# Four layer-1 weights and the centering matrix kept in SBUF for all images, in the room of one of two silu(z) buffers

## The chip, the core and the metric

The kernel runs on one core of a Trainium2 chip, as one program that handles all four images. The metric is the device time of that program in microseconds, the median of repeated runs. One execution was profiled; its trace gives every instruction of the five engines (TensorE = PE, VectorE = DVE, ScalarE = ACT, GpSimd = POOL, SyncE = SP) and the DMA packets.

## The reference

Four layers, applied one after the other to `x` of shape (4 images, 64, 64, 128), all in float32:

```python
# layer 0: four-direction selective scan (DI=256 channels, N=16 states, K=4 directions, L=4096 tokens)
xz = ln(x) @ in_proj;  x_, z = split(xz);  xc = silu(depthwise_conv3x3(x_) + conv_b)
# per direction k: delta, Bs, Cs are projections of xc
h = exp(delta*A) * h + (delta*xc) * B          # along 4096 tokens, per channel and state
y_k = sum_n(h * C) + D*xc                      # the four directions are summed
x = x + (ln(y) * silu(z)) @ out_proj;  x = x + fc2(gelu(fc1(ln(x))))
# layer 1: attention over all 4096 positions, softmax over the query axis
f, g, hv = x@Wq, x@Wk, x@Wv;  x = gamma * (hv^T @ softmax(f g^T, axis=1)) + x
# layer 2: 1x1 and 3x3 convolutions, batch norm, hard-swish, two residual blocks
# layer 3: 7x7 neighborhood attention, 4 heads, then an MLP
```

## The kernel before, in words

**Stages.** `scan_inputs` (lines 307 to 417) makes an image's inputs for the scan, in eight chunks of 512 tokens: layer norm, projection, convolution, `silu(z)` into the tile `sz` (line 389), `silu` of the convolution into `xc`, then `delta`, `B`, `C` and the product `du` (line 358, GpSimd). Each is stored to DRAM. `sz` is stored from ScalarE's DMA queue at line 412 and read back much later by `scan_output`.

`selective_scan` (487 to 611) runs the recurrence of an image, direction by direction. Its smallest step is a tile of 128 rows by 512 tokens: ScalarE makes `exp(delta*A)` (line 540, in PSUM), GpSimd makes `dB` (534, two tiles in one instruction), VectorE runs the recurrence with one scan instruction (542); the product with `C` is made by VectorE (547) or, for a fixed share of the units, by GpSimd (555); TensorE sums over states into `py` (588). An image has 1024 such VectorE scan instructions, the program 4096. This text counts progress in them: "scan 950" is the place before which 950 of them stand in VectorE's list.

`rest` (1721 to 1730) is everything else of an image: `scan_output` (gate, output projection and MLP of layer 0, together with the layer-3 MLP of the image before), `layer1`, `layer2`, `layer3_attention`. `rest` of image 0 runs during the scan of image 1, and so on. `rest` of image 3 has no scan beside it, and is built in a wider form that uses the scan's memory (`wide`): it is the last part of the program.

**What sets the order.** The kernel is written with the tile framework. The framework orders the instructions of each engine when the program is built, by priorities (`rest` goes ahead of the scan, which fills in) and by an estimate of when operands are ready (`TileContext(nc, schedule_with_timeline_sim=True)`). On the chip each engine then takes its list strictly in that order, and waits at an instruction whose operands are not there. DMA issues on SP stand in such a list too. So an edit in one place can shift how two stages interleave elsewhere.

**Memory.** Tiles come from pools. A pool opened later may lie where a closed pool lay, and a tile's first write then waits for the last use of what was there. `sz` in `scan_inputs` comes from a pool of two buffers.

**What the change touches.** In `scan_output`, each call makes the matrix `center` (identity minus 1/256, two 128x128 blocks, line 632) with a VectorE memset (633) and a VectorE add (634), and loads its weights; `out_proj_b` (631) is two VectorE products of the loaded weights; the first matmuls (651) use `center`, and the first VectorE work on their result is line 656. In `layer1`, each call loads `Wq`, `Wk`, `Wv` and `gamma` with the helper `load` (line 196, four DMA issues on SP) into the pool `l1_big`. The last VectorE instruction of a layer-3 attention tile is line 1443 (`x <- x, pj`), after line 1437 and ScalarE's lines 1414 (softmax exponentials), 1434 and 1435; line 1447 stores the result.

Of the kernel before, what the change touches and what calls it, by code (L numbers as in the profile page):

```python
# [28 lines left out]
F32 = mybir.dt.float32  # L29
# [7 lines left out]
B, H, W, C = 4, 64, 64, 128  # L37
NT = H * W
NJ = NT // 128
DI, NS, R, KD = 256, 16, 8, 4  # L40
ND = DI // 128
FF = 4 * C
NF = FF // 128
LC = 512
# [145 lines left out]
    return out  # L190


def loader(tc, pool, A, layer):
    def load(name, shape, src=None):
        t = pool.tile(shape, F32, name=f"w{layer}_{name}")
        tc.nc.sync.dma_start(t, A[f"L{layer}_conv_{name}"] if src is None else src)
        return t

    return load
# [107 lines left out]
def scan_inputs(tc, K, A, D, img):  # L307
# [4 lines left out]
    nc = tc.nc  # L312
    with ExitStack() as ctx:
        pool = ctx.enter_context(tc.tile_pool(name="si_a", bufs=2))
        wpool = ctx.enter_context(tc.tile_pool(name="si_aw", bufs=1))
        psum = ctx.enter_context(tc.tile_pool(name="si_ap", bufs=4, space=PSUM))
        load = loader(tc, wpool, A, 0)
# [46 lines left out]
        for c in range(NCH + 1):  # L364
            acts = []
            if c < NCH:
                xt = pool.tile([128, 4, 128], F32, name="x")
                nc.sync.dma_start(xt, token_tiles(A["x"][img], c))
                xnT = pool.tile([128, LC], F32, name="xnT")
                layernorm_T(tc, K, pool, psum, xt, ln_w, ln_b, xnT)  # L370
                band = pool.tile([128, ND, RC + 2, W], F32, name="band", bufs=3)
                bands[c] = band
                for d in range(ND):
                    ps = psum.tile([128, LC], F32, name="ps")
                    nc.tensor.matmul(ps, in_proj[:, d * 128 : (d + 1) * 128], xnT, start=True, stop=True)
                    rows = ps.rearrange("p (h w) -> p h w", w=W)
                    nc.scalar.copy(band[:, d, 1 : RC + 1, :], rows)
                    if c > 0:
                        nc.scalar.copy(bands[c - 1][:, d, RC + 1, :], rows[:, 0, :])
                        nc.scalar.copy(band[:, d, 0, :], bands[c - 1][:, d, RC, :])  # L380
                sz = pool.tile([128, ND, LC], F32, name="sz")
                for d in range(ND):
                    ps = psum.tile([128, LC], F32, name="ps")
                    mm = nc.tensor.matmul(
                        ps, in_proj[:, DI + d * 128 : DI + (d + 1) * 128], xnT, start=True, stop=True
                    )
                    if d == 0:
                        together.open(mm)
                    acts.append(lambda d=d, ps=ps, sz=sz: nc.scalar.activation(sz[:, d, :], ps, AF.Silu))
            if c > 0:  # L390

                b, src = c - 1, bands.pop(c - 1)
                top, bottom = (1 if b == 0 else 0), (RC + 1 if b == NCH - 1 else RC + 2)
                for d in range(ND):
                    ps = psum.tile([128, LC], F32, name="ps")
                    mm = conv3x3(
                        nc,
                        ps.rearrange("p (h w) -> p h w", w=W),
                        lambda t, d=d: diag[:, d, t, :],
                        src[:, d, top:bottom, :],  # L400
                        1 - top,
                        RC,
                        bottom - top,
                    )
                    acts.append(
                        lambda d=d, ps=ps, b=b: nc.scalar.activation(
                            xc[:, d, span(b)], ps, AF.Silu, bias=conv_b[:, d : d + 1]
                        )
                    )
            together.run(mm, acts)  # L410
            if c < NCH:
                nc.scalar.dma_start(D.sz[img][c], sz)
            if c > 0:
                nc.scalar.dma_start(D.xc[img][c - 1], xc[:, :, span(c - 1)])
                steps(0, c - 1)
# [198 lines left out]
def scan_output(tc, K, A, D, img, xT, last, scan_over=None):  # L614
# [5 lines left out]
    nc = tc.nc  # L620
    with ExitStack() as ctx:
        side = "left" if scan_over is None else "right"
        pool = ctx.enter_context(tc.tile_pool(name="so", bufs=2, side=side))
        wpool = ctx.enter_context(tc.tile_pool(name="so_w", bufs=1, side=side))
# [4 lines left out]
        out_proj_b = wpool.tile([128, ND, C], F32, name="out_proj_b")  # L629
        for d in range(ND):  # L630
            nc.vector.tensor_scalar_mul(out_proj_b[:, d, :], out_proj[:, d, :], onorm_b[:, d : d + 1])
        center = wpool.tile([128, ND, 128], F32, name="center")
        nc.vector.memset(center, -1.0 / DI)
        nc.vector.tensor_add(center[:, 0, :], center[:, 0, :], K.ident)
        ln_w, ln_b = load("ln2_w", [128, 1]), load("ln2_b", [128, 1])
        P = load_mlp(load)
        together = Together(tc, K)
# [126 lines left out]
def layer1(tc, K, A, D, img, xT, wide):  # L764
# [6 lines left out]
    with ExitStack() as ctx:  # L771
        big = ctx.enter_context(tc.tile_pool(name="l1_big", bufs=1))
        pool = ctx.enter_context(tc.tile_pool(name="l1", bufs=1))
        psum = ctx.enter_context(tc.tile_pool(name="l1_p", bufs=1, space=PSUM))
        load = loader(tc, big, A, 1)
        Wq, Wk, Wv = load("Wq", [128, 32]), load("Wk", [128, 128]), load("Wv", [128, C])
        gamma = load("gamma", [128, 1])
        L1 = SimpleNamespace()
        L1.f = f = big.tile([128, 2, LC], F32, name="l1_f")
        L1.g = g = big.tile([128, NCH, LC], F32, name="l1_g")  # L780
# [970 lines left out]
def network(tc, A, out):  # L1751
    nc = tc.nc
    with ExitStack() as ctx:
        nc.scalar.preload_act_table_set("natural_log_exp_and_others")
        K = make_consts(ctx, tc)
        dram = ctx.enter_context(tc.tile_pool(name="scratch", bufs=1, space=DRAM))

        def scratch(name, shape, kind=F32):
            return dram.tile(shape, kind, name=f"{name}_dram")

        D = SimpleNamespace()
        D.bias = scratch("bias", [len(BIAS_KINDS), 128, HEADS * 512])
        D.biasT = [[scratch(f"biasT{k}_{i}", [128, HEADS, LC]) for i in range(4)] for k in range(3)]
        D.T = scratch("T", [128, HEADS * (2 * KW - 1) + 1, W])
        D.conv_diag = scratch("conv_diag", [128, ND, 9, 128])
        D.w2_norms = scratch("w2_norms", [128, len(NORMS2), 4])
        D.w2_cv4, D.w2_bias = scratch("w2_cv4", [128, 128]), scratch("w2_bias", [3, 128], BF16)
        for name, shape in (("sz", [128, ND, LC]), ("xc", [128, ND, LC]), ("y", [128, ND, LC])):
            setattr(D, name, [[scratch(f"{name}{b}_{c}", shape) for c in range(NCH)] for b in range(B)])
        for name, shape in (("delta", [128, ND, LC]), ("du", [128, ND, LC]), ("bc", [NS, 2, LC])):  # L1770
            made = [
                [[scratch(f"{name}{b}_{k}_{c}", shape) for c in range(NCH)] for k in range(KD)] for b in range(B)
            ]
            setattr(D, name, made)
        D.y_first = [[[scratch(f"y_first{b}_{k}_{c}", [128, ND, LC]) for c in range(NCH)] for k in range(2)] for b in range(B)]
        D.y_cols = [scratch(f"y_cols{b}", [NCH, 128, NCH, ND, RC * RC]) for b in range(B)]
        for name in ("x4", "x5"):
            setattr(D, name, [scratch(f"{name}_{b}", [NT, C]) for b in range(B)])
        D.shift = [scratch(f"shift{b}", [NJ, 128]) for b in range(B)]

        with ExitStack() as scan_ctx:
            S = make_scan(scan_ctx, tc, K, A)
            make_conv_diagonals(tc, K, A, D.conv_diag)
            with priority(tc, K, SCAN_FIRST // 2):
                with tc.tile_pool(name="mk_w2", bufs=1, side="right") as pool:
                    make_layer2(tc, K, A, D, pool)
            scan_inputs(tc, K, A, D, 0)
            before = None
            for img in range(B):
                with priority(tc, K, SCAN_FIRST):  # L1790
                    selective_scan(tc, K, S, D, img)
                if img == 0:
                    make_bias(tc, K, A, D)
                    for later in range(1, B):
                        scan_inputs(tc, K, A, D, later)
                    more = scan_ctx.enter_context(tc.tile_pool(name="ss_more", bufs=1))
                    S.products.widen(more, 4)
                    S.inputs.widen(more, 1)
                else:
                    rest(tc, K, A, D, img - 1, before)  # L1800
                    before = img - 1, out[img - 1]
            rest(tc, K, A, D, B - 1, before, scan_ctx.close, out[B - 1])
        needed = ctx.enter_context(tc.tile_pool(name="needed", bufs=1)).tile([1, 1], mybir.dt.int32, name="needed")
        bound_exceeded(tc, K, needed)
        with tc.If(nc.values_load(needed) > 0):
            everything_again(tc, K, A, D, out)
# [80 lines left out]
```

## Time and profile before

| | us |
|---|---|
| median of 3 runs (8716.36 to 8720.45) | 8719.03 |
| the profiled execution's own time | 8713.75 |
| its span, first to last instruction | 8712.4 |
| PE busy (share of the span) | 6971.9 (80%) |
| DVE busy | 7095.9 (81%) |
| ACT busy | 5688.0 (65%) |
| POOL busy | 7119.3 (82%) |

The mean granted TensorE clock was 0.865. A page of the profile gives busy times by engine, the span in 40 equal slices, the chain of work that ended last, and the costliest groups of instructions; the trace answers questions on windows, waits and single instructions. In a row of the timeline the first number is the start in us from the span's start, the second the duration, and what stands in brackets is how long the engine had been idle and what released it. In a row of windows, each engine's busy time within the window is followed by its number of instructions; the last three numbers are the granted TensorE clock, the busy share of the DMA engines and their GB/s. A short name such as `w_fc_w` stands for several tiles, because numbers in names are left out.

### The profile page before, as it was taken

What the parts mean: (1) busy time and instruction counts of PE and PEld (TensorE: products, weight loads), DVE (VectorE), ACT (ScalarE), POOL (GpSimd) and SP (SyncE); (2) the same over time, 40 slices, a digit from 0 to 9 for tenths busy, and PEclk for the clock granted to TensorE, in tenths of its full rate; (3) what the DMA queues carried; (4) which work ended last, traced back from release to release, by engine and by line L of the source; (5) the groups of instructions that cost most, each with busy time, mean ns of one, the idle gap of its engine ahead of it and who ended that gap; (6) DMA issues with size and microseconds to landing.
All of it is one profiled execution on the core that took longest, in us unless ns stands there. A gap on an engine that the chain in (4) does not pass through costs nothing. (4 is left out here: it accounts for less than half of the span.)

```text
span 8712.4 us, 101929 instructions
## 1 busy us (share of the span) xinstructions
PE 6971.9 (80%) x30468; PEld 2615.3 (30%) x30468; DVE 7095.9 (81%) x8477; ACT 5688.0 (65%) x11652; POOL 7119.3 (82%) x3112
## 2 busy tenths in 40 slices
PE   6758587786788878777798877777899877888978
PEld 2223132222422222233322222234322223344333
DVE  4788787788899999998899999998899999913433
ACT  5657676675666676667766676667766766654366
POOL 6989999898899989998899989998899989900000
PEclk8868687787899988888899988888999988899989
DMA  5776667676555556565455566565455565520020
GB/s 181 254 261 236 244 235 257 227 261 220 172 176 167 170 190 206 190 223 186 162 180 169 171 197 201 192 225 176 164 172 168 180 204 196 191 73 5 0 84 11
DMA packets 859647, 1562.73 MB, mean 179 GB/s; under 512 B 224446, under 2 KB 342348, under 8 KB 856781
## 3 DMA queue, kind: packets, MB, share of 16 engines
q1 hardware_dynamic: 728781, 1379.94, 47.8%
q10 hardware_dynamic: 130304, 176.19, 5.7%
q8 instruction: 244, 4.00, 0.2%
q14 instruction: 318, 2.61, 0.1%
HBM read 1286.51 MB, written 281.92 MB: 180 GB/s over the span
## 5 line engine op out<-in xcount | busy, mean ns | idle before, releaser
L534 POOL TENSOR_TENSOR dB<-du,b_rows 128x1024 f32<-128x1024 f32 x2048 | 4797.9, 2367 | 374.9 <-DVE hc L542 95.0
L540 ACT ACTIVATE dA<-dt,w_A_log 128x512 f32<-128x512 f32 x4096 | 2778.3, 690 | 509.9 <-DVE hc L542 256.7
L542 DVE TENSOR_TENSOR_SCAN dA<-dA,state,dB 128x512 f32<-128x512 f32 x2072 | 2559.9, 1272 | 295.9 <-POOL dB L534 140.4
L555 POOL TENSOR_TENSOR hc<-hc,c_rows 128x1024 f32<-128x1024 f32 x864 | 2045.3, 2367 | 73.4 <-issue 22.2
L542 DVE TENSOR_TENSOR_SCAN hc<-dA,state,dB 128x512 f32<-128x512 f32 x1512 | 1871.9, 1267 | 281.8 <-ACT dA L540 123.5
L547 DVE TENSOR_TENSOR hc<-dA,c_rows 128x512 f32<-128x512 f32 x2368 | 1522.6, 675 | 31.8 <-PE py L588 13.9
L588 PE MATMUL py<-hc,pick 128*32 128x512 f32 x8192 | 1231.0, 675 | 261.5 <-POOL hc L555 235.4
L549 ACT COPY state<-dA 128x1 f32<-128x1 f32 x2072 | 318.6, 158 | 1170.8 <-DVE hc L547 1158.9
L878 PE MATMUL pa<-e,l_v 128*128 128x512 f32 x2048 | 1069.5, 654 | 16.6 <-ACT e L834 16.1
L830 PE MATMUL pair<-l_g,l_f 32*128 32x512 f32 x2048 | 533.3, 670 | 172.6 <-ACT e L834 130.6
L834 ACT ACTIVATE e<-pair 128x1024 f32<-128x1024 f32 (+1 forms) x448 | 508.5, 1135 | 234.4 <-PE pair L830 228.0
L1019 POOL MEMSET l_h<- 64x128 f32 x8 | 1.6, 196 | 707.9 <-DVE l_h L993 707.9
L878 PEld LDWEIGHTS pa<-e,l_v 128*128 128x128 f32 x2048 | 376.3, 200 | 673.9 <-issue 624.4
L588 PEld LDWEIGHTS py<-hc,pick 128*32 128x32 f32 x8192 | 212.1, 115 | 996.5 <-issue 467.5
L277 PE MATMUL ps<-band,w_conv_diag 128*128 128x504 f32 (+3 forms) x1152 | 501.9, 595 | 6.4 <-ACT delta L427 5.7
L1404 PE MATMUL pair<-table,ident 128*128 128x512 f32 x768 | 397.3, 641 | 91.7 <-ACT e L1414 63.3
L231 PE MATMUL ps<-ident,ln_xn 128*128 128x128 f32 x512 | 144.4, 375 | 327.6 <-ACT ln_xn L228 243.9
L542 DVE TENSOR_TENSOR_SCAN dA<-dA,dB 128x512 f32<-128x512 f32 x296 | 348.2, 1211 | 45.8 <-ACT dA L540 22.0
L358 POOL TENSOR_TENSOR du<-delta,xc 128x1024 f32<-128x1024 f32 x128 | 333.4, 2614 | 47.7 <-ACT delta L427 46.7
L1414 ACT ACTIVATE e<-pair 128x1024 f32<-128x1024 f32 (+1 forms) x224 | 254.3, 1135 | 95.8 <-PE pair L1408 95.5
L277 PEld LDWEIGHTS ps<-band,w_conv_diag 128*128 128x128 f32 x1152 | 221.1, 193 | 288.0 <-issue 261.1
L830 PEld LDWEIGHTS pair<-l_g,l_f 32*128 32x128 f32 x2048 | 140.0, 189 | 530.2 <-ACT e L834 258.9
(297 smaller groups left out, 8674.4 us busy)
## 6 DMA issues: line engine op xcount, KB each, us to landing
b_rows<-bc_dram SPq DMA_DIRECT2D x1024, 256.0 KB
c_rows<-bc_dram SPq DMA_DIRECT2D x1024, 256.0 KB
dt<-delta_dram SPq DMA_DIRECT2D x512, 512.0 KB
du<-du_dram SPq DMA_DIRECT2D x512, 512.0 KB
delta_dram<-delta ACTq DMA_DIRECT2D x128, 512.0 KB
du_dram<-du SPq DMA_DIRECT2D x128, 512.0 KB
table<-biasT_dram SPq DMA_DIRECT2D x72, 512.0 KB
y_first_dram<-y_sum ACTq DMA_DIRECT2D x128, 256.0 KB
```

The costliest lines, as they stand in the source:

```text
L277: mm = nc.tensor.matmul(out[:, r0 - row0 : r1 - row0, c0:c1], lhsT((dy + 1) * 3 + dx + 1), src[:, r0 + dy : r1 + dy, c0 + dx : c1 + dx], s ...
L358: nc.gpsimd.tensor_mul(du.rearrange("p d (a b) -> p d a b", b=H), deltas[b].rearrange("p d (a b) -> p d a b", b=H), tk,)
L534: nc.gpsimd.tensor_mul(dB, dus[pp], mid(bt, 2))
L540: nc.scalar.activation(dA, dts[pp][:, g, :], AF.Exp, scale=S.A[:, k, j, pr, g : g + 1])
L542: nc.vector.tensor_tensor_scan(hg[:, order], dA[:, order], dB[:, g, order], 0.0 if i == 0 else state[:, j, pr, g : g + 1], ALU.mult, ALU.add,)
L547: mm = nc.vector.tensor_mul(hc[:, g, :], dA, ct)
L555: made.append(nc.gpsimd.tensor_mul(hc, hc, mid(ct, 2)))
L588: mm = nc.tensor.matmul(py[0][32 * q : 32 * q + 32, :], S.pick, hcs[q // 2][:, q % 2, :], start=(k == 1 and j == 0), stop=(j == NJS - 1),)
L830: nc.tensor.matmul(ps[:, u, :], f[quad, t // 4, span(t % 4, 128)], g[quad, c, :], start=True, stop=True)
L834: made = nc.scalar.activation(e, ps, AF.Exp)
L878: nc.tensor.matmul(pa, v[:, 8 * q + t, :], es[q], start=(t == 0 and q == 0), stop=(t == 7 and q == 3),)
L1404: nc.tensor.matmul(ps[:, u, :], K.ident, t[:, u, :], start=True, stop=False)
```

## The change

`center`, `Wq`, `Wk`, `Wv` and `gamma` are made or loaded once, right after the constants, into a pool that stays open for the whole program. `layer1` and `scan_output` use these tiles. In `scan_inputs`, `sz` has one buffer where it had two: 4096 bytes a partition are given back there, and the new pool takes 2180 (1024 for `center`, 1156 for the four weights).

```diff
+def make_resident(ctx, tc, K, A):
+    pool = ctx.enter_context(tc.tile_pool(name="resident", bufs=1))
+    K.center = pool.tile([128, ND, 128], F32, name="center")
+    tc.nc.vector.memset(K.center, -1.0 / DI)
+    tc.nc.vector.tensor_add(K.center[:, 0, :], K.center[:, 0, :], K.ident)
+    load = loader(tc, pool, A, 1)
+    shapes = (("Wq", [128, 32]), ("Wk", [128, 128]), ("Wv", [128, C]), ("gamma", [128, 1]))
+    K.l1_weights = [load(name, shape) for name, shape in shapes]
...
 def scan_inputs(tc, K, A, D, img):
...
-                sz = pool.tile([128, ND, LC], F32, name="sz")
+                sz = pool.tile([128, ND, LC], F32, name="sz", bufs=1)
...
 def scan_output(tc, K, A, D, img, xT, last, scan_over=None):
...
-        center = wpool.tile([128, ND, 128], F32, name="center")
-        nc.vector.memset(center, -1.0 / DI)
-        nc.vector.tensor_add(center[:, 0, :], center[:, 0, :], K.ident)
+        center = K.center
...
 def layer1(tc, K, A, D, img, xT, wide):
...
-        load = loader(tc, big, A, 1)
-        Wq, Wk, Wv = load("Wq", [128, 32]), load("Wk", [128, 128]), load("Wv", [128, C])
-        gamma = load("gamma", [128, 1])
+        Wq, Wk, Wv, gamma = K.l1_weights
...
 def network(tc, A, out):
...
         K = make_consts(ctx, tc)
+        make_resident(ctx, tc, K, A)
```

## The prediction

> **What bounds the kernel now.** First the page's busy line, then the trace in windows. The boundaries are mine: the first gating product of `scan_output` (VectorE, line 656) of images 0, 1 and 2 at 2075.9, 3878.0 and 5802.1 us, then the end of the last scan, then the first gating product of image 3. The seventh and eighth windows cut stage 2's `layer1` and layer-3 attention out.
>
> ```profile
> PE 6971.9 (80%) x30468; PEld 2615.3 (30%) x30468; DVE 7095.9 (81%) x8477; ACT 5688.0 (65%) x11652; POOL 7119.3 (82%) x3112
> ```
>
> ```profile
> 0.00:2075.90 2075.90, 1455.07 (x4566) 514.10 (x4566) 1568.22 (x1863) 1356.07 (x3069) 1876.02 (x837) 0.78 0.70 239
> 2075.90:3878.00 1802.10, 1486.70 (x6978) 540.83 (x6978) 1695.57 (x1964) 1196.27 (x2447) 1717.50 (x745) 0.88 0.57 187
> 3878.00:5802.10 1924.10, 1577.88 (x7302) 571.07 (x7302) 1786.60 (x2096) 1306.44 (x2688) 1814.71 (x786) 0.89 0.57 187
> 5802.10:7623.00 1820.90, 1522.56 (x6987) 563.82 (x6988) 1683.92 (x1987) 1252.26 (x2577) 1710.32 (x741) 0.89 0.55 182
> 7623.00:7676.10 53.10, 35.49 (x184) 12.74 (x182) 3.72 (x15) 8.55 (x11) 0.00 (x0) 0.84 0.29 83
> ...
> 2375.00:3057.00 682.00, 607.94 (x2493) 186.10 (x2491) 648.04 (x687) 457.69 (x888) 679.70 (x295) 0.94 0.52 173
> 3232.00:3852.00 620.00, 487.45 (x2726) 180.35 (x2724) 588.55 (x668) 402.50 (x863) 609.88 (x264) 0.84 0.64 210
> ```
>
> POOL is busy for 7119 of the 7623 us in which it has work, and for 98 to 100% in the two long windows of stage 2 (the last number before the clock); its 85 us of idleness in that stage lie around them. A scan (one of the 4096 VectorE scan instructions) costs POOL (4797.9 + 2045.3) / 4096 = 1.67 us, by the page's groups of lines 534 and 555. So the time is: POOL's work for the scan and its idle gaps, to 7623; a stretch without a scan, 53 us; the rest of image 3, 1036 us.
>
> The 53 us, in the timeline of VectorE and then of SP:
>
> ```profile
> 7621.29 1.26 DVE L547 TENSOR_TENSOR hc<-dA,c_rows 128x512 f32<-128x512 f32 x2
> 7622.47 0.67 DVE L1443 TENSOR_TENSOR x<-x,pj 128x512 f32<-128x512 f32 x1
> 7654.68 0.69 DVE L1437 TENSOR_TENSOR oT<-rec,po 128x512 f32<-128x512 f32 x1 [31.54 <-ACT rec L1435]
> 7656.62 0.69 DVE L1443 TENSOR_TENSOR x<-x,pj 128x512 f32<-128x512 f32 x1 [1.25 <-PE pj L1441]
> ```
>
> ```profile
> 7657.34 0.38 SPq L1447 DMA_DIRECT2D x_dram<-x  x1
> 7659.76 0.33 SPq L196 DMA_DIRECT2D w_onorm_w<-in_L_conv_onorm_w  x1
> ...
> 7663.93 0.43 SPq L641 DMA_DIRECT2D y<-y_dram  x1
> ```
>
> The scan ends at 7622.5, but the last attention tile of image 2 ends at 7657.3. Its store holds the memory of the last `scan_output`, whose weights are issued from 7659.8 and whose first `y` from 7663.9. So an attention tile that is left over when the scan ends stands on the path.
>
> Then the add that makes `center`, and GpSimd beside it:
>
> ```profile
> 2050.08 11.21 DVE L634 TENSOR_TENSOR center<-center,ident 128x128 f32<-128x128 f32 x1
> ```
>
> ```profile
> 2049.62 6.93 POOL L534 TENSOR_TENSOR dB<-du,b_rows 128x1024 f32<-128x1024 f32 x3
> 2056.52 2.33 POOL L555 TENSOR_TENSOR hc<-hc,c_rows 128x1024 f32<-128x1024 f32 x1
> 2058.81 2.33 POOL L534 TENSOR_TENSOR dB<-du,b_rows 128x1024 f32<-128x1024 f32 x1
> 2063.80 2.45 POOL L534 TENSOR_TENSOR dB<-du,b_rows 128x1024 f32<-128x1024 f32 x1 [2.66 <-DMA w_ln_w<-in_L_conv_ln_w]
> ```
>
> The same add takes 0.29 us at 7660, where POOL is idle. Here it ends at 2061.29, 0.15 us after the last of five POOL instructions without a gap. At 3858.4 it takes 8.82 us and at 5780.4 7.42 us, again until 0.1 to 0.2 us after POOL's row of instructions breaks off. POOL then stands idle for 2.66, 1.48 and 2.65 us, since VectorE had consumed nothing.
>
> **Part by part.** The four loads go first on SP, ahead of all others. An issue takes 0.34 to 0.43 us at a pitch of 0.46: 4 x 0.46 = 1.9 us. The loads behind them lead to GpSimd's 20.8 us power (line 922, from 9.1), then to the weights at 38.6 and the first `xnT` at 41.4, with nothing slack: +1.9, bounds 0 and +3. The new memset and add (0.27 and 0.29 us) lie in VectorE's idle time, which lasts to 1.68 and has 0.92 us before 3.08; without that cover they cost 0.6, inside the bound.
>
> The single `sz`: ScalarE now waits at line 389 for the previous store. By the packets of ScalarE's DMA queue the 512 KB are through 2.3 to 8.0 us after the issue, and the next `silu(z)` comes 20.9 us or more after it (mostly 33 to 43). So 0. If that cover went, the scan's `exp` (line 540) would stand behind the wait on ScalarE, and VectorE and POOL behind that: at a landing of 30 us the four shortest gaps (20.9, 22.2, 25.1, 26.3) would lose 26 us.
>
> The twelve layer-1 issues that vanish from the scans take 12 x 0.46 = 5.5 us of SP, which waits for others most of the time; the last four went at 7636, inside the stretch without a scan. One TensorE wait of 9.4 us for `w_Wq` (image 0) vanishes too, in a stage where POOL sets the pace: 0, bound -9.
>
> The three stretched adds: 11.21 + 8.82 + 7.42 = 27.45 us, and 6.0 us of waits before the memsets. But in the new lists `out_proj_b` (line 631) becomes VectorE's first instruction in the new memory. It waits for the store of the last attention tile, three issues and a load, with only some 6.6 us of scan work between: I estimate 3 us of waiting each time, 10 in all. VectorE wins 33 - 10 = 23 us; POOL at least keeps going where it lost 2.66 + 1.48 + 2.65 = 6.8 less what the new waits cost it. I take -10, near the row of POOL's own idleness, with bounds -2 and -23. The Trainium skill, "SBUF — State Buffer", sections "Who interferes with whom" and "Summary: rules for kernel authors", says that a VectorE instruction with two SBUF inputs blocks until a GpSimd instruction that reads SBUF has finished. By that the adds would have lost one instruction each, 3 x 2.4 = 7 us, and this term would be -7; here they lost three to five, which no sentence there says, and the measured rows decide.
>
> The order. The lists of the built programs hold the same instructions apart from the removed ones, interleaved anew. First gating products stand before scan 950, 1978, 3067 in the old list, before 962, 1964, 3034 in the new: the four stages hold 950, 1028, 1089, 1029 scans before and 962, 1002, 1070, 1062 after. The last attention tile: in the old list seven of its eight exponentials (line 1414) and 54 TensorE instructions stand behind the last scan work, in the new list none of TensorE's, and on VectorE only lines 1437 and 1443. So the 7656.62 + 0.69 = 7657.3 becomes the scan's end at 7622.5 plus about 3: -32. But the new list gives that tile 28 scans where others have 44 to 49. Alone it needs 8 x 4.5 = 36 us of TensorE (the seven above ran from 7622 to 7653), with the `py` of 28 scans (1231 / 4096 x 28 = 8) 44 us, against 47 of POOL: nearly full, so I give 4 back: -28, bounds -32 and -18. Behind it the same store, weights and `y` are next; the lists of the last 1036 us are otherwise nearly equal.
>
> Sum: +1.9 + 0 + 0 - 10 - 28 = -36. The profiled execution, 8713.75, is 5 under the median; 8719 - 36 = **8683**.
>
> **The rivals.** That the change doesn't do what it says is excluded by the lists: four loads and one `center` remain in the path that runs.
>
> *More*: all of VectorE's 23 us come back, with 32 for the tile and 9 for `w_Wq`: 8719 + 2 - 64 = 8657. For it: VectorE is 92 to 94% busy in stages 2 to 4; against: POOL is ahead of it there.
>
> *No change*: each stage is as long as its chain of `rest`, whatever number of scans lies within. Then the old 1821 + 33 us of stage 4 stay and hold 1062 scans, and only adds and loads count: 8719 - 10 + 2 = 8711. For it: in `scan_output` POOL is 17 to 19% idle (252 busy of 310 us in image 0, 354 of 427 in image 1), so something else sets the pace; against: the 98 to 100% of the long windows, and the same `scan_output` with the MLP taking 244 us without a scan (7670 to 7914) and 427 with one.
>
> *Slower*: stages 1 and 4, which get 12 + 33 scans more, grow by 45 x 1.67 = 75 us, while stages 2 and 3, which get 26 + 19 fewer, keep their length, held by `rest` on TensorE (608 of 682 us in `layer1`, which loses 24 scans in image 1): 8719 + 75 - 32 - 10 + 2 = 8754. In my forecast stages 2 and 3 give back the 75; below 39 of them the kernel is slower than before. For it: TensorE's 89%; against: `layer1` took 666 us (4294 to 4960) with image 1's 432 scans and 656 (6234 to 6890) with image 2's 416, so it does shorten with them.
>
> **How the numbers follow.** Forecast 0.62, more 0.12, no change 0.15, slower 0.11. A measurement can tell about 0.2%, 17 us: 8701.6 and 8736.5. Forecast and more are faster (0.74), no change is the same (0.15), the last slower (0.11). The range takes in the forecast with all its bounds (-64 to -17), with it more, and most of no change: 8652 to 8714.
>
> **What would show it.** Right: the add for `center` once, before 5 us, and no VectorE instruction of 7 us in the scans; first gating products near 2095, 3851, 5740 if POOL sets the pace; the scan's end near 7614 with line 1443 within 5 us of it; the store at line 412 before the next line 389. Wrong: line 1443 over 15 us after the scan's end, POOL idle for more than 85 and 109 us in stages 2 and 3, or a scan that ends past 7640.

## The result, and the profile after

The changed kernel takes 8706.6 us (median of 20 runs, 8697.4 to 8713.2), the kernel before in the same comparison 8720.3 (20 runs): a ratio of 0.9983, 95% interval 0.9976 to 0.9990, about 14 us less. The forecast was 36 less. The profiled executions span 8712.4 before and 8703.6 after, 8.8 us apart: the one before lies some 6 us under its kernel's median, the one after 1. Idle times and places below are of one execution each.

The line numbers are higher now: by 10 up to `out_proj_b` (631 is 641; 534, 542, 547, 555 are 544, 552, 557, 565), by 8 at the first gating product (656 is 664), by 6 in the attention (1443 is 1449). First the page's busy line, then the windows, cut as before at the first gating products, the end of the last scan and the first gating product of image 3.

```profile
PE 6941.6 (80%) x30468; PEld 2596.8 (30%) x30468; DVE 7108.7 (82%) x8471; ACT 5688.5 (65%) x11652; POOL 7118.1 (82%) x3112
```

```profile
0.00:2114.50 2114.50, 1473.94 (x4598) 514.58 (x4601) 1590.53 (x1883) 1366.54 (x3093) 1895.28 (x846) 0.77 0.69 237
2114.50:3878.50 1764.00, 1456.83 (x6927) 529.58 (x6926) 1656.47 (x1922) 1176.28 (x2401) 1672.66 (x726) 0.90 0.57 187
3878.50:5776.00 1897.50, 1553.07 (x7243) 573.63 (x7244) 1763.14 (x2059) 1293.33 (x2666) 1786.43 (x775) 0.89 0.57 186
5776.00:7643.60 1867.60, 1549.77 (x7222) 562.00 (x7220) 1737.81 (x2044) 1282.71 (x2628) 1762.92 (x764) 0.90 0.56 183
7643.60:7664.30 20.70, 9.17 (x32) 3.82 (x33) 2.98 (x14) 1.25 (x3) 0.00 (x0) 0.67 0.69 196
```

POOL's work is the same (7118.1 for 7119.3), but it stands idle for 2114.5 - 1895.3 = 219.2 us in the first stage (199.9 before), then for 91.3 and 111.1 (84.6 and 109.4). The gating products come at 2114.5, 3878.5 and 5776.0, where the forecast had 2095, 3851 and 5740, and the scans end at 7643.6 and not near 7614. Only the stretch without a scan did what was forecast: 20.7 us where it had 53.1. Its timeline on VectorE:

```profile
7642.36 1.27 DVE L557 TENSOR_TENSOR hc<-dA,c_rows 128x512 f32<-128x512 f32 x2
7643.55 0.68 DVE L1443 TENSOR_TENSOR oT<-rec,po 128x512 f32<-128x512 f32 x1
7645.48 0.69 DVE L1449 TENSOR_TENSOR x<-x,pj 128x512 f32<-128x512 f32 x1 [1.25 <-PE pj L1447]
```

The last attention tile ends 2.5 us after the scans, where it ended 34.8 after them. So the span's 8.8 us are: scans' end +21.0, tile -32.3, everything behind the tile +2.4.

**What became of the stretched add.** `center` is added once, in the prologue. In its place, VectorE's `out_proj_b`, with GpSimd beside it:

```profile
2088.64 2.46 DVE L552 TENSOR_TENSOR_SCAN hc<-dA,state,dB 128x512 f32<-128x512 f32 x2 [1.48 <-POOL dB L544]
2092.18 10.53 DVE L641 TENSOR_SCALAR out_proj_b<-w_out_proj_w,w_onorm_b 128x128 f32<-128x128 f32 x2 [1.08 <-DMA w_out_proj_w<-in_L_conv_out_proj_w]
2102.63 2.45 DVE L552 TENSOR_TENSOR_SCAN dA<-dA,state,dB 128x512 f32<-128x512 f32 x2
```

```profile
2090.87 2.33 POOL L565 TENSOR_TENSOR hc<-hc,c_rows 128x1024 f32<-128x1024 f32 x1
2093.17 6.95 POOL L544 TENSOR_TENSOR dB<-du,b_rows 128x1024 f32<-128x1024 f32 x3
2100.09 2.33 POOL L565 TENSOR_TENSOR hc<-hc,c_rows 128x1024 f32<-128x1024 f32 x1
2105.22 2.35 POOL L544 TENSOR_TENSOR dB<-du,b_rows 128x1024 f32<-128x1024 f32 x1 [2.79 <-DMA sz<-sz_dram]
```

The first of the two multiplications takes 10.33 us of the 10.53, and ends 0.09 us after GpSimd's row of five instructions breaks off; the same at 3854.6 (10.90 us) and 5753.6 (13.18). Together 34.4 us, where the three adds had taken 27.45; GpSimd then stands for 2.79, 3.39 and 2.80 us. Why this line (631 there) looked harmless shows in the timeline of the kernel before:

```profile
2061.22 2.45 DVE L542 TENSOR_TENSOR_SCAN hc<-dA,state,dB 128x512 f32<-128x512 f32 x2
2063.59 0.45 DVE L631 TENSOR_SCALAR out_proj_b<-w_out_proj_w,w_onorm_b 128x128 f32<-128x128 f32 x2
```

It began at 2063.59, inside the gap (2061.14 to 2063.80) that the stretched add had made. The add paid for both.

**Where the scans' 21 us arise.** GpSimd's idle time (the sum of the gaps between its instructions) is 17.1 us above that of before already at 350 us, 105.6 against 88.5, and 23.0 above at its last scan instruction. Its first rows, before and after:

```profile
81.55 2.35 POOL L358 TENSOR_TENSOR du<-delta,xc 128x1024 f32<-128x1024 f32 x1 [45.22 <-ACT delta L427]
84.68 2.34 POOL L358 TENSOR_TENSOR du<-delta,xc 128x1024 f32<-128x1024 f32 x1 [0.79 <-ACT delta L427]
102.41 2.34 POOL L534 TENSOR_TENSOR dB<-du,b_rows 128x1024 f32<-128x1024 f32 x1 [15.39 <-DMA du<-du_dram]
```

```profile
83.52 4.65 POOL L368 TENSOR_TENSOR du<-delta,xc 128x1024 f32<-128x1024 f32 x2 [45.41 <-ACT delta L437]
107.70 2.35 POOL L544 TENSOR_TENSOR dB<-du,b_rows 128x1024 f32<-128x1024 f32 x1 [19.53 <-DMA du<-du_dram]
```

The first `du` is 2.0 us late, as the four issues were priced; the first `dB` is 5.3 late. SP's queue stands in another order there: after, all four `dt` loads go ahead of the `du` loads that `dB` needs.

```profile
88.56 1.60 SPq L517 DMA_DIRECT2D dt<-delta_dram  x2
...
95.35 1.26 SPq L517 DMA_DIRECT2D du<-du_dram  x2
```

```profile
97.47 1.28 SPq L527 DMA_DIRECT2D dt<-delta_dram  x2
99.18 3.78 SPq L527 DMA_DIRECT2D du<-du_dram  x4
```

The first fence is before, the second after: `du` is first issued at 95.35 and at 99.18, so 3.8 of the 5.3 us lie ahead of that issue and 1.5 behind it. Four GpSimd gaps follow by 318 us, 23.9 us together; the kernel before has only two over 3 us there (3.50 and 5.32):

```profile
149.01 2.36 POOL L544 TENSOR_TENSOR dB<-du,b_rows 128x1024 f32<-128x1024 f32 x1 [6.54 <-issue]
205.69 2.36 POOL L544 TENSOR_TENSOR dB<-du,b_rows 128x1024 f32<-128x1024 f32 x1 [4.04 <-PE ps L345]
281.85 2.35 POOL L544 TENSOR_TENSOR dB<-du,b_rows 128x1024 f32<-128x1024 f32 x1 [7.12 <-PE ps L345]
318.11 2.35 POOL L544 TENSOR_TENSOR dB<-du,b_rows 128x1024 f32<-128x1024 f32 x1 [6.20 <-PE py L598]
```

What GpSimd waits for in these gaps is not settled by the names: e10 below has the same four, and the profile names others for two of them.

### The profile page after: what moved, and what is told of

Same layout as the page of the kernel before. It is cut to its first block, busy times and chain, and to the rows that moved or that the text cites. A ratio compares the mean times of both kernels' runs of the same rounds, so it can differ in the third digit from the quotient of the medians.

```text
span 8703.6 us, 101904 instructions
## 1 busy us (share of the span) xinstructions
PE 6941.6 (80%) x30468; PEld 2596.8 (30%) x30468; DVE 7108.7 (82%) x8471; ACT 5688.5 (65%) x11652; POOL 7118.1 (82%) x3112
## 5 line engine op out<-in xcount | busy, mean ns | idle before, releaser
L565 POOL TENSOR_TENSOR hc<-hc,c_rows 128x1024 f32<-128x1024 f32 x864 | 2072.1, 2398 | 88.2 <-ACT state L561 26.1
```

Of the source, the lines that this page charges most:

```text
L565: made.append(nc.gpsimd.tensor_mul(hc, hc, mid(ct, 2)))
```

## The experiments

Two theories besides the forecast's: *the stall moved* (the resident `center` is worth nothing, since `out_proj_b` takes over the wait), and *the order* (the new interleaving of the lists gives the gain at the last tile and takes some back in the first 350 us). All ratios are against runs of the kernel before on the same chip. "Idle" is GpSimd's, up to 350 us and up to its last scan instruction; "tile" is the end of the last attention tile (its line 1443) less the end of the scans (the last product of line 547). us, from each run's trace:

| kernel | ratio, 95% interval | idle to 350 | idle in all | scans end | tile |
|---|---|---|---|---|---|
| before | | 88.5 | 503.1 | 7622.6 | +34.8 |
| changed | 0.9983, 0.9976 to 0.9990 | 105.6 | 526.1 | 7643.6 | +2.5 |
| e1 single `sz` | 1.0001, 0.9991 to 1.0010 | 87.5 | 505.7 | 7624.9 | +34.8 |
| e2 and `center` | 1.0012, 1.0003 to 1.0021 | 88.4 | 512.1 | 7631.3 | +35.0 |
| e3 `sz` and weights | 0.9980, 0.9971 to 0.9989 | 103.4 | 520.2 | 7638.3 | +2.5 |
| e4 changed, `out_proj_b` on ScalarE | 0.9967, 0.9955 to 0.9979 | 107.1 | 507.4 | 7625.8 | +2.5 |
| e5 before, both on ScalarE | 0.9982, 0.9973 to 0.9991 | 86.2 | 484.2 | 7603.4 | +34.8 |
| e6 four extra early loads | 1.0013, 1.0004 to 1.0022 | 107.3 | 532.8 | 7650.9 | +16.3 |
| e7 loads late | 0.9973, 0.9962 to 0.9984 | 90.3 | 500.4 | 7620.7 | +14.4 |
| e8 loads late, ScalarE | 0.9949, 0.9935 to 0.9962 | 88.3 | 483.9 | 7605.8 | +14.4 |
| e9 changed, source in PSUM | 0.9957, 0.9944 to 0.9971 | 105.9 | 507.5 | 7626.1 | +3.4 |
| e10 loads on ScalarE's queue, ScalarE | 0.9930, 0.9916 to 0.9943 | 103.7 | 487.1 | 7606.6 | -1.2 |

**e1: the single buffer alone.**

```diff
-                sz = pool.tile([128, ND, LC], F32, name="sz")
+                sz = pool.tile([128, ND, LC], F32, name="sz", bufs=1)
```

> The kernel before with one buffer for the inputs' silu(z) and nothing else; its instruction lists are those of before. Both theories: no change, within 0.1% (9 us), and no wait of ScalarE over 1 us at the silu(z) for the previous store. A third theory, that the single buffer is what puts 17 us of idle time on GpSimd in the first 350 us of the changed kernel, expects +15 to +20 us and gaps there.

8721.4 against 8721.5, and GpSimd's idle time at 350 us is that of before. In the trace ScalarE waits at line 389 for TensorE alone, never for the previous store. No cost of the buffer shows, and it is not what made the first 350 us longer.

**e2: the resident `center`, weights loaded per image.** e1 and the first four lines of `make_resident`, with `center = K.center` in `scan_output`.

> One silu(z) buffer and the resident center, with the four layer-1 weights still loaded for every image, so that everything but the removed memsets and adds stays in the order of before. The prediction's theory (out_proj_b, which now comes first, waits some 3 us each time): 10 us less than before, 2 to 23. The theory that the stall only moves: out_proj_b takes 8 to 13 us three times where it took 0.27, together within 5 us of the three adds' 27.4 us, GpSimd breaks off behind each for 2 to 3.4 us as before, and the time is that of before within 5 us.

8730.0 against 8721.5. The list is that of before, the adds are gone, and nothing is won. The timeline of VectorE shows the stall in its new place:

```profile
2055.07 11.46 DVE L638 TENSOR_SCALAR out_proj_b<-w_out_proj_w,w_onorm_b 128x128 f32<-128x128 f32 x2
```

It took 11.26 us here and 8.69 and 4.79 in the next two images, 24.7 in all. The forecast's -10 is refuted, since the whole interval lies above 1. Whether this part by itself loses some us is open: its interval overlaps that of e1, though GpSimd's idle time is 6.4 us above e1's.

**e3: the resident weights, `center` built per image.** e1, the pool and the last three lines of `make_resident`, with `layer1` using them.

> One silu(z) buffer and the resident layer-1 weights, with center built anew for every image: the interleaving of the changed kernel, with the adds of before. If the whole gain of the change is the order's: 14 us less than before, within 5 us of the changed kernel; the adds take 7 to 13 us, out_proj_b 0.3. By the prediction's theory the resident center is worth 10 of the gain, so this is 10 us slower than the changed kernel, 4 less than before. Last attention tile within 5 us of the end of the scans.

8706.4, the changed kernel's 8706.6. The whole gain belongs to the weights, and through them to the order: it has the same interleaving, the same loss in the first 350 us and the same tile. The adds are stretched to 10.49, 11.96 and 4.37 us, 26.8 in all. `out_proj_b`, 0.25 to 0.28 us where GpSimd stands, began once beside a running GpSimd instruction (at 3861.96) and was itself held, for 2.06 us.

**e4: the changed kernel without the stall.**

```diff
-            nc.vector.tensor_scalar_mul(out_proj_b[:, d, :], out_proj[:, d, :], onorm_b[:, d : d + 1])
+            nc.scalar.activation(out_proj_b[:, d, :], out_proj[:, d, :], AF.Copy, scale=onorm_b[:, d : d + 1])
```

> The changed kernel with out_proj_b computed by ScalarE, so that neither the add nor the multiplication stands on VectorE; every other instruction in the order of the changed kernel. If the stretched VectorE instruction costs what GpSimd then loses behind it (2.79 + 3.39 + 2.80): 9 us less than the changed kernel, 5 to 12. If all of VectorE's 34.4 - 0.8 us count: 34 less. If GpSimd makes it up from elsewhere: no change within 4 us. On ScalarE the multiplication takes under 1 us.

8693.4, 13 less than e3, which stands for the changed kernel in the same comparison (by their ratios to before, e4 lies 14 under the changed kernel). The profile's group of the line on ScalarE:

```profile
L641 ACT ACTIVATE out_proj_b<-w_out_proj_w,w_onorm_b 128x128 f32<-128x128 f32 x8 | 2.8, 393 | 8.4 <-DMA w_out_proj_w<-in_L_conv_out_proj_w 5.9 <-DMA y_dram<-y_sum 2.5
```

0.39 us each. Three stalls on VectorE, 27 to 34 us together, are worth 13 to 14 us of time; GpSimd's idle time falls by 18.7 (526.1 to 507.4), more than the 9.0 us of gaps right behind the stalls and far less than VectorE's 34.

**e5: the same in the kernel before.** e4's edit, and `center` made by two ScalarE copies (`bias=-1.0 / DI`, the second with `scale=0.0`).

> The kernel before, with center and out_proj_b built by ScalarE in place of VectorE; loads, buffers and the order of all else are those of before. If the stretched add is worth the same 13 us here as the stretched multiplication was in the changed kernel (8706.6 against 8693.4): 13 less than before, 8 to 18. If it costs only what GpSimd stands idle behind it (2.66 + 1.48 + 2.65): 7 less. If the 13 us belong to the changed kernel's order alone: no change within 4 us.

8699.6 against 8715.7: 16 less with the order of before, GpSimd's idle time 18.9 less. So a true removal of the stalls is worth 13 to 16 us in either order. The forecast's size for it, 10 with a bound of 23, was fair; the change just doesn't remove them.

**e6: four early loads that nobody reads.** e2, with the four loads of `make_resident` added and `layer1` left as it was.

> One silu(z) buffer, the resident center, the four early loads of the weights, but the per-image loads are kept and used, so that the four early ones are four issues more on SP and nothing else. The lists are interleaved anew from TensorE's 75th instruction on, as in the changed kernel, and 14 scans stand beside the last attention tile. Theory that the four issues ahead of all others turn the order of the first scans for the worse: GpSimd's idle time is 12 to 20 us above that of before at 350 us, as in the changed kernel. Theory that it comes from the removed per-image loads: as in before within 4 us. The tile should end within 8 us of the scans, and the time be 8 to 20 us under before.

8723.5 against 8715.7. The idle time at 350 us is 18.8 us above before's: the early issues bring it, not the removed loads. On the time this was a miss: I had credited the shorter tile and not debited the idle time. The tile's end came 18.5 us nearer to the scans' end, but the scans ended 28.3 later.

**e7: the same resident loads, issued late.**

```diff
-    K.l1_weights = [load(name, shape) for name, shape in shapes]
+    with priority(tc, K, 2 * SCAN_FIRST):
+        K.l1_weights = [load(name, shape) for name, shape in shapes]
```

> The changed kernel with the four resident loads at a low priority, so that SP issues them late: lists as before through image 0's stage, the new order only from the middle of the third stage, 16 scans beside the last attention tile. If the first 350 us are what the changed kernel lost: no 17 us there, the end of the scans near 7625, the tile within 8 us of it, and 10 to 20 us less than the changed kernel, 24 to 34 under before. If the idle time only comes later (each stage's chain takes its own time): as the changed kernel within 5 us.

8693.8 against 8715.7, 22 less where 24 to 34 were expected. With the order of before in the first two stages the loss is gone (90.3 at 350 us), and the scans end at 7620.7. The tile ends 14.4 us after them, not within 8: beside 0, 14, 16 and 28 scans it ended 34.8, 16.3, 14.4 and 2.5 us after the last. By a straight line through these, an estimate, each scan that is left to it is worth (34.8 - 2.5) / 28 = 1.2 us, and 16 are too few.

**e8: e7 and e4 together.**

> The last kernel with out_proj_b on ScalarE as well. If the two effects are independent: another 13 us less than the kernel with the late loads, some 40 under before. If the late loads give nothing: as the changed kernel with out_proj_b on ScalarE, 28 under before. If GpSimd is no longer what sets the pace after the first step: under 5 us from the second.

8672.5, 21 less than e7 and 43 under before: the two effects add up, the second being larger here than the 13 to 16 us of e4 and e5, for a reason that was not traced (GpSimd's idle time is 16.5 less than e7's).

**e9: the multiplication on VectorE, from PSUM.**

```diff
+            pw = psum.tile([128, C], F32, name="ps")
+            nc.tensor.matmul(pw, K.ident, out_proj[:, d, :], start=True, stop=True)
-            nc.vector.tensor_scalar_mul(out_proj_b[:, d, :], out_proj[:, d, :], onorm_b[:, d : d + 1])
+            nc.vector.tensor_scalar_mul(out_proj_b[:, d, :], pw, onorm_b[:, d : d + 1])
```

> The changed kernel with out_proj_b left on VectorE at the same place, but its input is first copied to PSUM by TensorE (two products with the identity per image), so that VectorE reads PSUM where it read SBUF; all else in the order of the changed kernel. If what is held is a VectorE instruction that reads SBUF alone beside a GpSimd that reads SBUF (the products with dA in PSUM show no such stretch in the trace): under 0.5 us each, the time within 5 us of the variant with ScalarE, 13 less than the changed kernel. If VectorE is held at that place whatever it reads: 8 to 13 us three times and no change within 4 us of the changed kernel.

8689.1, a ratio of 0.9957 where e4 has 0.9967; the intervals overlap. The trace's answer for the line (shortest, median and longest in ns):

```profile
L643 DVE TENSOR_SCALAR out_proj_b<-ps,w_onorm_b x8: 324/349/352, 2096.6 to 7636.5; 128x128 f32<-128x128 f32 x8
```

The same operation at the same place is not held once its source lies in PSUM: all six in the scans began while GpSimd was busy, and GpSimd's row ran on for 15 to 21 us behind them without a break. This fits the Trainium skill, "SBUF — State Buffer", section "Who interferes with whom": a VectorE instruction with at most one SBUF input, outside the two-port modes, does not contend with GpSimd, while `tensor_scalar` can enter such a mode.

**e10: time or order, and the best version.** e4 with the loads on another queue:

```diff
-    load = loader(tc, pool, A, 1)
...
+        t = pool.tile(shape, F32, name=f"w1_{name}")
+        tc.nc.scalar.dma_start(t, A[f"L1_conv_{name}"])
```

> The changed kernel with the four resident loads on ScalarE's queue (so that SP's first issues are those of before) and out_proj_b on ScalarE. The order is that of the changed kernel up to TensorE's 188th instruction, from there its own: 946, 1012, 1074 and 1064 scans, 28 of them beside the last attention tile. If the 1.9 us of early issues cause the loss in the first 350 us: GpSimd's idle time there within 4 us of before, the tile within 5 us of the scans' end, and some 12 us less than the best so far (8672), 8655 to 8665. If the order causes it: idle 12 to 19 us above before again, and 8685 to 8697, as the changed kernel with out_proj_b on ScalarE.

SP's first issues are no longer delayed, and the first `du` comes 1.6 us earlier than in the kernel before, yet GpSimd's next row waits as long as in the changed kernel:

```profile
79.94 4.65 POOL L370 TENSOR_TENSOR du<-delta,xc 128x1024 f32<-128x1024 f32 x2 [43.73 <-ACT delta L439]
104.13 2.35 POOL L546 TENSOR_TENSOR dB<-du,b_rows 128x1024 f32<-128x1024 f32 x1 [19.54 <-DMA du<-du_dram]
```

`du` is first issued at 95.60 here, 0.25 us later than in the kernel before, and the first `dB` is still 1.7 us late; the four later gaps stand at the same places (7.15, 6.25, 7.14 and 7.04 us). GpSimd's list is the changed kernel's up to 256 us, but VectorE's differs from 143 us on, so the split is not clean. At 350 us the idle time is 15.2 above before's: some 15 of the 17 belong to the order, some 2 to the issue time. The time does not go with the theory of the order: 8666.8 against 8727.6 is 61 us less, where the theory of the issue time gave 51 to 61 under its own before, 8715.7, and that of the order 25 to 36 (e4's place, with its before, 8721.5). From its own part of the order on GpSimd loses less (idle 71.6 us in the second stage, 87.5 in e4; 13 of the 16 us lie in the first 200 us, the time of `scan_output`), and the tile ends before the scans. Which waits of the new order that spares is open. By its ratio it is the fastest version that was run, though its interval just touches that of e8.

## Why the prediction was right or wrong

- **The bound** held as a way to count: GpSimd's work stays as it was (7119.3 and 7118.1 us), so the scans' end moves with its idle time, and that and the tile move the total. That 27 to 34 us of VectorE's time were worth 13 to 16 speaks for it too. It does not say where the idle time comes from.
- **Prologue +1.9**: the first `du` came 2.0 late. **Single `sz`, 0**: e1. **The twelve loads, 0**: not measured by themselves; in e3 they go together with the new order, and the tile (-32.3) and the scans' end (+15.7) account for its span (-15.9).
- **The removed add, -10, failed**, in the step "I estimate 3 us of waiting each time". It priced `out_proj_b`'s wait for its load, and gave its run time no price, as it ran for 0.25 and 0.27 us before. But that row stood in GpSimd's gap behind the add. Once it comes first it is stretched itself, for 34.4 us where the add lost 27.45. The term measured 0 (e3 equals the changed kernel within the intervals; e2 is not faster). The page of the Trainium skill that the prediction cites, "SBUF — State Buffer", names `tensor_scalar` in the same section as an operation that can contend as well; I applied its rule to the add alone.
- **Order and tile, -28**: the tile's part was right, 32.3 of 32. The 4 us given back were for that tile, and were not needed. What failed is that the rest of the new order stood at nothing in the sum: the stages were to trade 75 us of scans against 75, and GpSimd's idle time was to change by the prologue and the adds alone. The scans end 21.0 us later in place of about 8 earlier, and GpSimd's idle time is 17 us higher already by 350 us. I had looked at the number of scans in each stage and not at what GpSimd waits for in the new list. That the early loads bring this loss is shown (e6 has it, e7 has not); what GpSimd waits for in each gap stays open.
- The sum, term by term, becomes +2 (prologue), 0, 0, 0 (add), -32 (tile), +19 (the scans' end without the prologue's 2), +2 behind the tile: -9, as in the two spans; the medians are 14 apart.
- **The rivals.** *No change* lies nearest with its 8711, but its mechanism fell: the stages follow their scans. The first stage is 38.6 us longer with 12 scans more, the next two 38.1 and 26.6 shorter with 26 and 19 fewer. That also refutes *slower*: stages 2 and 3 give back 64.7 of the 75 us, where 39 decide. (One premise against it was misread: in the two `layer1` stretches, 4294 to 4960 and 6234 to 6890, the trace of before has 401 and 396 scans, not 432 and 416.) *More* needed VectorE's 23 us in full; e4 shows that 27 to 34 of them are worth 13 to 14.
- Of the signs named beforehand, no VectorE instruction of 7 us, the gating times and the scans' end failed; GpSimd's idle time over 85 and 109 us and a scan past 7640 said wrong. The tile's sign held.

## What to carry to other kernels

Before you count a removed stall as won, find the next instruction that meets the same condition; a row that looks cheap behind the stall may be cheap only because the stall emptied the other engine. Move such small preparations to an engine, or a source, that isn't held: here ScalarE or a PSUM source, 13 to 16 us for one line or two. Where a scheduler makes the order, four early loads can re-interleave a program: read the new list's first rows, not only its totals, and try other places or queues for the loads.

## What the runs showed of the hardware

A held VectorE instruction did not wait for one GpSimd instruction but for the end of an unbroken row of them. In the 21 cases of seven kernels (the adds of before, e1 and e3, the first multiplications of the changed kernel, e2, e6 and e7) it took 4.37 to 13.18 us, two to six GpSimd instructions ended in that time, and it ended 0.08 to 0.15 us after the last, when GpSimd had run out of work. In all 21 GpSimd then stood for 1.48 to 3.39 us, and started again 0.13 to 0.15 us after the first or second scan that VectorE then finished, which fits a wait for VectorE to use up what GpSimd had made. Both forms are held, the add with two SBUF tiles as inputs and the multiplication of one SBUF tile by per-partition scalars. The 2313 products with `dA` in PSUM (line 547, kernel before) that began while GpSimd was busy took 0.63 to 0.72 us.

The change leaves held instructions of another stage in place: line 188, with SBUF inputs of three partitions, takes 0.33 us where GpSimd stands, and took 2.50 and 2.51 us in the changed kernel at 3261.6 and 5135.5, ending 0.14 us after a GpSimd instruction each time.
